# Two graph layers over 16 batches: the list path of the kernel issued in text order

## The chip, the core and the metric

The kernel runs as one program on one core of a Trainium2 chip. The metric is the device time of one execution in microseconds (us). The engines are called by the names of the profile: PE (matmuls; PEld is its weight load), DVE (the vector engine), ACT (the scalar engine), POOL (GpSimd, which here only issues indirect DMAs: gathers and scatters of rows by a list of row numbers) and SP (which issues the plain DMAs).

## The reference

There are B = 16 batches of N = 1024 nodes with C = 64 channels, and a weighted adjacency of 1024 x 1024 for each batch, with self-loops; its expected degree falls with the node's number. Both layers begin with a layer norm and a relu, and add their result to x. Layer 0 is a mean over neighbours weighted by the adjacency. Layer 1 removes some neighbours of nodes with more than ten (each k-th one, in both directions), takes for each node and channel the weighted 0.25, 0.5 and 0.75 quantiles over the neighbours that are left, adds the node's own value, and applies a perceptron of 64, 128 and 64 channels.

```python
h = relu(layernorm(x))
x = x + matmul(adj / clip(sum(adj, 2), 1), h)          # layer 0
h = relu(layernorm(x))                                  # layer 1
adj_d = dilate(adj)            # nodes with over 10 neighbours lose each skip-th
sv = sort(where(adj_d > 0, h of neighbours, big))       # per node and channel
agg = 0.25 * q(0.25) + 0.5 * q(0.5) + 0.25 * q(0.75)    # interpolated quantiles
x = x + (relu((h + agg) @ W1 + b1) @ W2 + b2) * mask
```

## The kernel before, in words

**Layer 0 (a batch at a time).** `front` (L303) norms x, and for each of eight blocks of 128 rows loads the block of the adjacency (L329, 512 KB, tile `at`), takes its signs on ACT (L331), turns them on DVE into numbered marks (L332, L333) and finds the eight largest of each of four segments with MAX8 (L336): these are the neighbour lists, in `rec`. PE transposes the block (L341), ACT copies it out of PSUM (L342). `product` (L356) multiplies half a batch by h (16 matmuls, L358), ACT copies the result (L363) and PE turns it back; it runs inside block 4 and at the start of `back`. `back` (L382) writes the new h to the table `tab` and to `own` in DRAM, sorts the nodes by degree (L408 to L433) and permutes the lists by matmuls with one-hot tiles (L438, L444) into `rec_g`.

**Lists of a group.** A group is four batches. `group` (L652) lays the permuted lists on 128 partitions (nodes of like degree together, 31 columns), makes the neighbour indices, and writes for the largest nodes what was dropped (scatters at L757). It then makes ten jobs, one for each list length from 15 down to 1 (L768). `long_lists` (L777) does the same for the four classes of longest lists (88, 31, 24 and 20 neighbours), over all batches, after a gather of whole adjacency rows (`lat`).

**A job** has T columns of nodes with n = length + 1 places each. `fetch` (L611) issues T x n gathers on POOL (L481): the node's own row into `S`, and each neighbour's row into the tile `places` (`lplaces` for the long lists). `sort` runs `aggregate` (L486) on DVE: it marks what was removed (`rem`, `gone`, `ok`, L491 to L502), makes the quantile weights (`wu` on DVE, two ACT instructions L472 and L473, then `w` on DVE, L476), sorts by a network of minimum and maximum operations (L531) and multiplies by the weights (L544, tile `prod`). `layers` is the perceptron: PE (L572), ACT (L577), PE (L579), ACT (L581), PE (L585, L588), ACT into `y` (L590). `add` (L629) adds x on DVE, `store` (L593) scatters T rows of the output from POOL (L595). `pipeline` (L634) runs step s: fetch of job s + 2, stores of job s - 2, layers of job s - 1, sort of job s, add of job s - 1. A job's tile `places` has three buffers.

**Order.** The program is written as Python generators that yield an estimated cost; `weave` (L850) takes its next piece from the stream that has used the smallest share of its weight. But this text order is only a priority: the framework's scheduler then reorders each engine's instructions by its own model, and each engine runs its queue in that order. A sort is cut into pieces of about 8 us by estimate (L520). Groups 0 and 1 are woven with layer 0; when layer 0 is over, groups 2 and 3 are woven with the long lists (L901 to L907).

Of the kernel before, what the change touches and what calls it, by code (L numbers as in the profile page):

```python
# [1 line left out]

# [5 lines left out]
F32 = mybir.dt.float32  # L8
# [17 lines left out]
GB = 4  # L26
# [11 lines left out]
WAIT = "wait"  # L38
AHEAD = 2
# [77 lines left out]
def kernel(  # L117
# [26 lines left out]
    list_path(tc, x, adj, nodemask, w1, b1, w2, b2, out, go)  # L144
# [7 lines left out]
def list_path(ctx, tc, x, adj, nodemask, w1, b1, w2, b2, out, go):  # L152
# [27 lines left out]
    diff = consts.tile([P, P], I32, name="diff")  # L180
# [23 lines left out]
    place1 = consts.tile([P, P], F32, name="place1")  # L204
    nc.vector.tensor_scalar(place1, col[:, :P], 1.0, None, op0=OP.add)
    cls_i = consts.tile([P, CLS, NT], I32, name="cls_i")
# [46 lines left out]

    first = keep.tile([REC, len(LONG), B, LSUB], HF, name="first")
# [40 lines left out]

    def load(pool, b):
# [6 lines left out]
    def front(pool, st, following):  # L303
# [17 lines left out]
        st["att"] = []  # L321
        for t in range(NT):
# [5 lines left out]
            at = pool.tile([P, N], F32, name="at", bufs=3)  # L328
            nc.sync.dma_start(at, adj[b, blk, :])  # L329
# [5 lines left out]
            for s in range(NSEG):  # L335
                nc.vector.max(out=rec[:, t, 8 * s:8 * s + 8], in_=segs[:, s, :])  # L336
            for h2 in range(2):
# [7 lines left out]
                )  # L345
            if t == BPH:
                product(pool, st, 0)
# [4 lines left out]
            yield 2.6  # L352
# [29 lines left out]
    def back(pool, st, rec_g):  # L382
# [5 lines left out]
        for _ in range(3):  # L388
            yield 0.0
# [45 lines left out]
        for hf in range(2):  # L435
            perm = pool.tile([P, NT, HALF], HF, name="perm", bufs=1)
            for t in range(NT):
# [3 lines left out]
                )  # L441
            pr = ps_m.tile([P, HALF], F32, name="pm")
# [14 lines left out]
            yield 2.9  # L457
# [28 lines left out]
    def aggregate(pool, n, T, A, S, keys, node):  # L486
# [32 lines left out]
        for op, ai, aj, dist, run in ops:  # L519
            if cost > 8.0:  # L520
                yield cost
                cost = 0.0
# [8 lines left out]
            nc.vector.tensor_tensor(dst, a, c, op)  # L531

# [6 lines left out]
        for copy in range(2):  # L539
            for run in runs_of([k for k in range(count) if at[k] == copy]):  # L540
# [6 lines left out]
                )  # L547
        yield cost + 0.4 + count * T * C * 1.05e-3
# [13 lines left out]
    def perceptron(terms, mask, T):  # L562

        R = terms[0][0].shape[1]
        y = mlp.tile([P, T, CO], F32, name="y", bufs=2)
# [27 lines left out]
    def store(y, T, idx):  # L593
        for t in range(T):
            ins = nc.gpsimd.indirect_dma_start(  # L595
                out=out_rows, out_offset=bass.IndirectOffsetOnAxis(ap=idx[:, t:t + 1], axis=0),
                in_=y[:, t, :], in_offset=None,
            )

            for other in scatters:  # L600
                tc.declare_no_dep(ins.ins, other, reason="rows of their own")
            scatters.append(ins.ins)

    class Job:


        def __init__(self, pool, n, T, keys, idx, node, mask, nodes_i, table, mine, name="places",
                     bufs=3):
            self.__dict__.update(locals())

        def fetch(self):  # L611
# [19 lines left out]
        def store(self):  # L631
            store(self.y, self.T, self.nodes_i)
# [566 lines left out]
```

## Time and profile before

| | us |
|---|---|
| median of 8 runs | 2077.95 |
| lowest and highest run | 2057.58 and 2094.01 |
| the profiled execution | 2065.86 |
| its span, first to last instruction | 2064.1 |
| DVE busy in the span | 1289.8 (62%), 4747 instructions |
| POOL busy | 1120.2 (54%), 940 instructions |
| PE busy, PEld | 868.7 (42%), 523.0 (25%) |
| ACT busy | 436.3 (21%) |

Busy is time in which the engine ran an instruction of the program; instructions of DVE overlap by some 70 ns, and what is counted is the union. POOL leaves 0.30 us between two DMA instructions that wait for nothing, so its busy share understates how full its queue is. In the lines, L481 is the line of the helper that issues every gather; `places<-tab,idx` are the gathers of group jobs (496), `lplaces<-tab,lidx` those of the long lists (163), `S<-own,nodes_i` the nodes' own rows (124 and 4), `out_dram<-y,nodes_i` the stores (124 and 4). "Remote" in a wait means that no instruction or DMA in the profile was seen to end it.

### The profile page before, as it was taken

What the parts mean: (1) busy time and instruction counts of PE and PEld (TensorE: products, weight loads), DVE (VectorE), ACT (ScalarE), POOL (GpSimd) and SP (SyncE); (2) the same over time, 40 slices, a digit from 0 to 9 for tenths busy, and PEclk for the clock granted to TensorE, in tenths of its full rate; (3) what the DMA queues carried; (4) which work ended last, traced back from release to release, by engine and by line L of the source; (5) the groups of instructions that cost most, each with busy time, mean ns of one, the idle gap of its engine ahead of it and who ended that gap; (6) DMA issues with size and microseconds to landing.
All of it is one profiled execution on the core that took longest, in us unless ns stands there. A gap on an engine that the chain in (4) does not pass through costs nothing.

```text
span 2064.1 us, 15523 instructions
## 1 busy us (share of the span) xinstructions
PE 868.7 (42%) x3724; PEld 523.0 (25%) x3724; DVE 1289.8 (62%) x4747; ACT 436.3 (21%) x1010; POOL 1120.2 (54%) x940
## 2 busy tenths in 40 slices
PE   6886256457773754479300010001225215121165
PEld 3443123233541422245100000001113104121044
DVE  9998588537777785677694111179656475555172
ACT  6663134123443432233100000000001100000011
POOL 0002637653327444742327777664888888378753
PEclk9997578567886876778555555555556556555566
DMA  6554244142344432331111111100111101000100
GB/s 198 157 154 116 59 113 124 37 117 66 89 113 103 118 96 64 103 86 24 35 45 25 27 27 27 25 15 9 25 21 22 22 11 23 13 20 15 32 17 14
DMA packets 116516, 124.32 MB, mean 60 GB/s; under 512 B 84242, under 2 KB 84370, under 8 KB 116418
## 3 DMA queue, kind: packets, MB, share of 16 engines
q1 hardware_dynamic: 85730, 84.15, 14.8%
q0 software_dynamic: 30688, 39.11, 9.1%
q8 instruction: 31, 0.51, 0.1%
q14 instruction: 67, 0.55, 0.1%
HBM read 106.27 MB, written 16.92 MB: 60 GB/s over the span
## 4 chain that ended last, share of the span: by engine, by line
POOL 25%; DVE 21%; PE 21%; issue 16%; another core or an unknown queue 8%; DMA 4%; ACT 3%; POOLq 0%; SPq 0%; DVEq 0%; ACTq 0%
POOL places L481 14%; PE pm L358 8%; POOL lplaces L481 7%; DVE other L531 4%; PE pm L444 4%; PE pt L341 4%; PE pt L572 2%; DVE places L531 2%; DVE rec L336 2%; POOL out_dram L595 2%; POOL S L481 2%; DVE lplaces L531 1%; DMA at<-in_adj_dram 1%; DMA places<-tab,idx 1%
## 5 line engine op out<-in xcount | busy, mean ns | idle before, releaser
L481 POOL DMA_INDIRECT places<-tab,idx x496 | 663.9, 1339 | 387.0 <-DVE prod L544 177.7
L572 PE MATMUL pt<-ident,prod 128*128 128x128 f32 (+1 forms) x736 | 160.0, 373 | 660.0 <-DVE prod L544 329.3
L572 PEld LDWEIGHTS pt<-ident,prod 128*128 128x128 f32 (+1 forms) x736 | 128.0, 254 | 702.7 <-issue 241.2
L358 PE MATMUL pm<-att,h 128*65 128x512 f32 x512 | 242.8, 621 | 3.3 <-issue 1.8
L595 POOL DMA_INDIRECT out_dram<-y,nodes_i x124 | 128.8, 1039 | 150.5 <-issue 53.3
L341 PE MATMUL pt<-ident,at 128*128 128x128 f32 x1024 | 164.8, 307 | 70.7 <-ACT att L342 27.4
L336 DVE MAX8 rec<-sg 128x8 f16<-128x256 f16 x512 | 188.7, 413 | 2.8 <-DVE base L430 1.1
L481 POOL DMA_INDIRECT lplaces<-tab,lidx x163 | 155.3, 953 | 49.7 <-issue 49.4
L481 POOL DMA_INDIRECT S<-own,nodes_i x124 | 145.0, 1169 | 60.3 <-issue 31.9
L331 ACT ACTIVATE sg<-at 128x1024 f16<-128x1024 f32 x128 | 135.8, 1061 | 154.8 <-DVE rec L336 112.3
L341 PEld LDWEIGHTS pt<-ident,at 128*128 128x128 f32 x1024 | 132.3, 158 | 112.0 <-issue 59.4
L342 ACT COPY att<-pt 128x512 f32<-128x512 f32 x256 | 141.0, 588 | 78.1 <-PE pt L341 36.2
L444 PE MATMUL pm<-perm,rec 128*34 128x512 f16 x256 | 98.1, 498 | 86.4 <-DVE perm L438 55.4
L531 DVE TENSOR_TENSOR places<-other 128x128 f32<-128x128 f32 (+6 forms) x264 | 86.6, 350 | 58.5 <-remote 54.1
L531 DVE TENSOR_TENSOR other<-places 128x128 f32<-128x128 f32 (+6 forms) x276 | 93.0, 350 | 35.5 <-remote 26.8
L590 ACT ACTIVATE y<-ps_small,recs 128x64 f32<-128x64 f32 x124 | 30.8, 313 | 372.5 <-DMA out_dram<-y,nodes_i 259.8
L579 PE MATMUL pm<-ot,w_sb 128*128 128x128 f32 (+3 forms) x112 | 51.5, 558 | 134.0 <-ACT ot L577 71.4
L358 PEld LDWEIGHTS pm<-att,h 128*65 128x65 f32 x512 | 69.8, 144 | 140.4 <-issue 133.5
L476 DVE TENSOR_TENSOR w<-wu 128x16 f32<-128x16 f32 (+12 forms) x44 | 7.7, 176 | 152.9 <-ACT wu L473 95.8
L481 POOL DMA_INDIRECT gat_rows<-in_adj_dram,nodes_i x4 | 4.0, 1012 | 178.3 <-DVE over L686 173.4
L629 DVE TENSOR_TENSOR y<-y,S 128x64 f32<-128x64 f32 (+4 forms) x44 | 15.1, 344 | 134.9 <-DMA out_dram<-y,nodes_i 69.8
L333 DVE TENSOR_TENSOR sg<-sg,rev 128x1024 f16<-128x1024 f16 x128 | 87.1, 683 | 12.0 <-issue 7.5
(194 smaller groups left out, 1687.6 us busy)
## 6 DMA issues: line engine op xcount, KB each, us to landing
at<-in_adj_dram SPq DMA_DIRECT2D x128, 512.0 KB
places<-tab,idx POOLq DMA_INDIRECT x496
tab<-h SPq DMA_DIRECT2D x16, 264.0 KB
xt<-in_x_dram SPq DMA_DIRECT2D x16, 256.0 KB
own<-x SPq DMA_DIRECT2D x16, 256.0 KB
own<-h SPq DMA_DIRECT2D x16, 256.0 KB
lplaces<-tab,lidx POOLq DMA_INDIRECT x163
S<-own,nodes_i POOLq DMA_INDIRECT x124
```

Source lines behind the costliest of these rows:

```text
L331: nc.scalar.activation(sg, at, AF.Sign, accum_out=total[:, t:t + 1])
L333: nc.vector.tensor_tensor(sg, sg, rev, OP.mult)
L336: nc.vector.max(out=rec[:, t, 8 * s:8 * s + 8], in_=segs[:, s, :])
L341: nc.tensor.transpose(pt[:, q * P:(q + 1) * P], at[:, c0:c0 + P], ident)
L342: nc.scalar.copy(att[:, h2 * BPH:(h2 + 1) * BPH, k * P:(k + 1) * P], pt.rearrange("p (q i) -> p q i", i=P),)
L358: nc.tensor.matmul(po[:C + 1, :], st["h0"][:, q, :], st["att"][hf][:, q, :], start=(q == 0), stop=(q == NT - 1),)
L444: nc.tensor.matmul(pr[:REC, :], rec[:, t, :], perm[:, t, :], start=(t == 0), stop=(t == NT - 1))
L481: nc.gpsimd.indirect_dma_start(out=dst, out_offset=None, in_=src, in_offset=bass.IndirectOffsetOnAxis(ap=idx, axis=0),)
L531: nc.vector.tensor_tensor(dst, a, c, op)
L572: nc.tensor.matmul(pt[:term.shape[1], i * P:(i + 1) * P], term, ident, start=(k == 0), stop=(k == len(terms[t]) - 1),)
L579: nc.tensor.matmul(ph[:, :M], w1_sb[:R, :], ot[:R, :M], start=True, stop=True)
L595: ins = nc.gpsimd.indirect_dma_start(out=out_rows, out_offset=bass.IndirectOffsetOnAxis(ap=idx[:, t:t + 1], axis=0), in_=y[:, t, :], in_of ...
```

## The change

The scheduler's reordering is switched off for the list path (`manual_schedule`): every engine issues its instructions in the order of the program's text. That order is written anew:

- Layer 0 yields after each MAX8; rows of the adjacency are loaded two blocks ahead, at the end of a block. `front` and `back` of neighbouring batches run by weights 24 and 14 instead of in turn.
- A sort yields after about 0.9 us of operations by estimate (`PIECE`) instead of 8. After each 0.8 us of sorting operations (`BREATH`) DVE gets a memset of one element per partition (`breathe`).
- The ten jobs of a group go into one queue for all groups, in an order that pairs long lists with short ones. One `pipeline` runs all 40. The cost of a piece of a sort is now counted in POOL's time: 1.27 us for each gather or store of the step, shared out over the sort's pieces.
- In a step the stores are dealt among the fetches (`transfers`), a store first; after a store with no fetches left POOL gets a small memset.
- The lists of a group have weight 0, which puts them before everything else as soon as four more batches are done. While layer 0 runs, the jobs of all groups that have lists are dealt against it at 730 to 480. When it is over come the lists of group 3, all four long lists, and then the long jobs against the rest of the group jobs at 440 to 300. The long jobs fetch two ahead.
- Some setup tiles share space, and `y` has three buffers instead of two.

```diff
+BREATH = 0.8
+PIECE = 0.9
...
-    list_path(tc, x, adj, nodemask, w1, b1, w2, b2, out, go)
+    with tc.manual_schedule():
+        list_path(tc, x, adj, nodemask, w1, b1, w2, b2, out, go)
...
+        def __call__(self, cost):
+            self.since += cost
+            if self.since > BREATH:
+                nc.vector.memset(idle, 0.0)
+                self.since = 0.0
...
                 nc.vector.max(out=rec[:, t, 8 * s:8 * s + 8], in_=segs[:, s, :])
+                if s < NSEG - 1:
+                    yield 0.9 if s == 0 else 0.42
...
+            if t + 2 < NT:
+                rows.append(load_rows(pool, b, t + 2))
+            elif following is not None:
+                following["rows"].append(load_rows(pool, following["b"], t + 2 - NT))
...
-            yield 2.6
+            yield 0.42
...
         product(pool, st, 1)
-        for _ in range(3):
-            yield 0.0
+        yield 4.0
...
+                if t % 2:
+                    yield 0.7
...
-            if cost > 8.0:
+            if cost > PIECE:
                 yield cost
                 cost = 0.0
...
             nc.vector.tensor_tensor(dst, a, c, op)
+            breathe(0.07 + len(run) * T * C * 1.05e-3)
...
-        y = mlp.tile([P, T, CO], F32, name="y", bufs=2)
+        y = mlp.tile([P, T, CO], F32, name="y", bufs=3)
...
+            self.cost = 2.5 + (2 * n * T * C * 1.05e-3) + sum(
+                0.15 + len(run) * T * C * 1.05e-3 for *_, run in network(n)[0]
+            )
...
+    def transfers(fetch, store):
+
+        fetch = list(fetch.fetches()) if fetch is not None else []
+        store = list(store.stores()) if store is not None else []
+        while fetch or store:
+            if store:
+                store.pop(0)()
+                if not fetch:
+                    nc.gpsimd.memset(turn, 0.0)
+            for _ in range(-(-len(fetch) // (len(store) + 1))):
+                fetch.pop(0)()
+
+    def pipeline(jobs, total, ahead, by_pool=True):
+
+
+        for s in range(-ahead, total + 2):
+            fetch = store = None
+            if s + ahead < total:
+                while len(jobs) <= s + ahead:
+                    yield WAIT
+                fetch = jobs[s + ahead]
+            if 0 <= s - 2:
+                store = jobs[s - 2]
+            time = 1.27 * ((fetch.n * fetch.T if fetch else 0) + (store.T if store else 0))
+            transfers(fetch, store)
+            if 1 <= s <= total:
                 jobs[s - 1].layers()
-            if s < J:
-                yield from jobs[s].sort()
-            if 1 <= s <= J:
+            if 0 <= s < total:
+                for cost in jobs[s].sort():
+                    yield time * cost / jobs[s].cost if by_pool else cost
+            else:
+                yield time if by_pool else 0.1
+            if 1 <= s <= total:
                 jobs[s - 1].add()
-            yield 0.2
+            if by_pool:
+                progress["sorted"] = max(s + 1, 0)
...
-        for ts in classes:
+
+        half = len(classes) // 2
+        mixed = [ts for pair in zip(classes[:half], classes[:half - 1:-1]) for ts in pair]
+        for ts in mixed + classes[half:len(classes) - half]:
...
-            yield from alternate(front(pool, st, following), ending)
+            yield from streams((front(pool, st, following), 24.0), (ending, 14.0))
...
+            while progress["batches"] < (g + 1) * GB or progress["sorted"] < (g - 1) * per_group:
                 yield WAIT
             yield from group(g, records[g])
-            yield from pipeline(todo[g], AHEAD)
+            progress["groups"] = g + 1
...
+        yield from long_lists(pool, 0)
+        while progress["groups"] < NG:
+            yield WAIT
+        for l in range(1, len(LONG)):
             yield from long_lists(pool, l)
...
-        weave((lay0, 480.0), (groups(records, (0, 1)), 270.0))
+        layer0 = batches(pool, records)
+        emit(layer0, lambda: progress["batches"] == GB)
+        emit(
+            streams((lists, 0.0), (layer0, 480.0), (jobs, 730.0)),
+            lambda: progress["batches"] == B,
+        )
     with tc.tile_pool(name="long", bufs=1) as pool:
-        def rest():
-            yield from group(2, records[2])
-            yield from group(3, records[3])
-            progress["dropped"] = True
-            yield from pipeline(todo[2] + todo[3], AHEAD)
-        weave((longs(pool), 440.0), (rest(), 270.0))
+        emit(streams(
+            (lists, 0.0), (longs(pool), 0.0),
+            (pipeline(long_jobs, len(LONG), 2, by_pool=False), 440.0), (jobs, 300.0),
+        ))
```

## The prediction

> **What bounds the kernel now.** I read first the table of busy times by stage: layer 0 of the first five batches, the rest of layer 0 with groups 0 and 1, and all that follows; then one stretch of the last.
>
> ```profile
> core 0: us, PE busy (x) PEld busy (x) DVE busy (x) ACT busy (x) POOL busy (x), PEclk, DMA share, GB/s
> 0.00:170.00 170.00, 138.54 (x612) 70.64 (x612) 156.92 (x565) 101.93 (x199) 1.91 (x9) 0.94 0.60 167
> 170.00:990.00 820.00, 498.25 (x2074) 273.75 (x2072) 573.58 (x2108) 270.18 (x602) 396.84 (x371) 0.75 0.34 87
> 990.00:2064.00 1074.00, 231.90 (x1042) 178.56 (x1041) 559.28 (x2075) 64.15 (x209) 721.43 (x561) 0.54 0.11 23
> 1140.00:1300.00 160.00, 11.89 (x36) 8.63 (x36) 23.00 (x113) 2.56 (x10) 121.30 (x128) 0.50 0.14 27
> ```
>
> No engine is full after 170 us. DVE is idle 246 us of the second stage (820 - 574) and 515 us of the third (1074 - 559). From 1140 to 1300 POOL gathers 128 rows of long lists in a train and DVE works 23 us of 160. The third stage, with half the group jobs and all the long lists, has the most to give.
>
> The timeline of POOL (start, duration) shows what sorting does to gathers, that of DVE what a train of gathers does to sorting:
>
> ```profile
> 1644.48 11.14 POOL L481 DMA_INDIRECT places<-tab,idx  x1 [0.30 <-DMA places<-tab,idx]
> 1655.92 13.70 POOL L481 DMA_INDIRECT places<-tab,idx  x1 [0.30 <-issue]
> 1669.93 7.39 POOL L481 DMA_INDIRECT places<-tab,idx  x1 [0.30 <-issue]
> ```
>
> ```profile
> 1148.73 0.29 DVE L531 TENSOR_TENSOR places<-other 128x128 f32<-128x128 f32 x1 [6.12 <-remote]
> 1150.13 0.29 DVE L531 TENSOR_TENSOR places<-other 128x128 f32<-128x128 f32 x1 [1.11 <-remote]
> ...
> 1154.33 0.15 DVE L281 TENSOR_SCALAR half<-half 128x1 int32<-128x1 int32 x1 [3.58 <-remote]
> 1155.73 0.16 DVE L284 TENSOR_TENSOR far<-far,lrec 128x1 f32<-128x1 f32 x1 [1.25 <-DVE half L281]
> ```
>
> An undisturbed gather takes 0.94 us and 0.30 to the next. These three lie under unbroken rows of two-input operations. In the second view DVE waits for its own earlier result (those waits are for its own semaphore), and gets it 1.4, 2.8 or 4.2 us late while gathers follow each other. The two engines shut each other out, and whoever is unbroken wins.
>
> Last the list of waits (total us, times, longest):
>
> ```profile
> ACT y L590 <- DMA out_dram<-y,nodes_i: 259.8, 12, 75.6
> ...
> DVE w L476 <- ACT wu L473: 95.8, 17, 21.7
> ...
> DVE y L629 <- DMA out_dram<-y,nodes_i: 69.8, 2, 51.3
> ...
> DVE w L476 <- ACT wu L472: 52.5, 4, 18.3
> ```
>
> Stores stand in POOL's queue behind fetches of later jobs, so `y` comes free late (first and third line); and DVE waits for the quantile weights behind whatever ACT has in front of them: with 4.6 from other causes 152.9 us over 44 jobs, 3.5 each.
>
> **The change, part by part.**
>
> *Work that stays, and what is added.* POOL keeps 923 gathers and stores and 8 scatters: 931 x 1.25 = 1164 us of queue if nothing shuts it out. DVE keeps 1290. Following the sorting networks through the rule of `breathe`, a group's jobs get 74 memsets and the long jobs 280: 576 in all. A memset of one element takes 0.059 us in the setup (L223): 34 us. POOL's memsets after last stores are a few tenths each: nothing.
>
> *The breath.* In the second stage, where MAX8 and other one-input work lies between the sorts, 248 `places` gathers took 263.2 us (1.06 each); from 1450 to 1900 us 141 took 265.6 (1.88). So an operation with one input lets gathers in, and a memset has none. I count gathers at 1.25 us again in the last stage. That matters only where POOL is last.
>
> The Trainium skill (SBUF — State Buffer, Who interferes with whom) has it that a DVE operation with two SBUF inputs holds only the pair's read side and, by inference, leaves descriptor writing alone. Then breaths would be 34 us for nothing. The 13.70 us gather speaks against it. The same section lets one-input operations outside the two-port modes pass GpSimd, as the 1.06 does.
>
> *First stage.* Five fronts and four backs, as before: DVE 157 us. In text order ACT's copy of `product` (L363) stands before the signs of the next block; PE needs 16 x 0.43 = 6.9 us for it, during which DVE has some 3 us of its own. I charge 4 us a batch: 170 + 20 = 190.
>
> *Second stage.* Layer 0 has 467 units of estimated cost left (11 fronts of 21.5, 12 backs of 19.2), so at 480 to 730 the jobs get 710 units of POOL's estimate, of 4 x 186 x 1.27 = 945: three quarters, and with fetches two steps ahead 28 jobs of 40 are sorted, eight more than now, and group 2's lists are made. By successive starts in the trace the 40 group sorts hold DVE 375 us (9.4 each), a group's lists 14, the long lists 67, the long sorts 264. So DVE has 574 + 8 x 9.4 + 14 + 207 breaths x 0.059 = 675 us; POOL 557 x 1.25 = 696. Neither covers the other, so what DVE waits for counts in full:
> - `w`. `layers` of the job before now always stands in ACT's queue before `wu`, and nothing of DVE between. For T = 4 that chain took in the trace 1482.2 (first PE) to 1492.9, then 0.9 for `y` and 0.6 for `wu`: 12 us; about 104 for the ten jobs of a group, 10.4 each. Layer-0 pieces that fall between the last product and the next step cover some 2, and ACT runs ahead of DVE. Between 3.5 (the row of waits) and 10.4 I take 4.5, nearer the row that was measured: 28 x 4.5 = 126.
> - Other layer-0 waits, 117 us now (sg, ln_v, base, perm, rec): finer pieces put other work between producer and consumer, text order takes away the freedom to pass: 60 (0 to 120).
> - Its own results and landings, 46 and 25 now: 40.
> Together 675 + 226 = 901, ending at 1091.
>
> *Third stage.* Group 3's lists and four long lists come first, 81 us of DVE. The gather of `lat` has one buffer, so the fourth goes out when DVE begins the third list, about 68 us in; behind it stand the 89 fetches of the first long job, 89 x 1.25 = 111: landed at 182. The first piece of that sort follows at once in DVE's text, so DVE idles some 85 us there. What is left on DVE then: 559 - 14 - 75 + 369 breaths x 0.059 - 81 = 411. POOL has 267 x 1.25 = 334 us meanwhile, hidden. Waits for `w`: 12 x 4.5 + 4 x 4 = 70. The stores that held `y` (70 on DVE) now go out two steps later at the head of a step: 0. The end, from the last product through perceptron, add, store and the final flag, is 15 us as now. Together 182 + 411 + 70 + 15 = 678.
>
> Sum: 190 + 901 + 678 = 1769 us of span, 1771 for the execution (2065.86 - 2064.1 lies around it). The profiled execution is 0.6% under the median; on the median's scale 1781. I say 1775.
>
> **The rivals.**
> 1. *Both engines stay full* (17%). If finer pieces hide the waits on ACT, the second stage is POOL's 696 or DVE's 675 plus little, 715, the first 175, the third 182 + 411 + 15 = 608: about 1500. For it: in the first stage DVE is already busy 157 of 170 us. Against it: nothing stands between `wu` and `w` in the text.
> 2. *The full chain is waited for* (15%): 10.4 us for 40 jobs instead of 4.5 adds 236: 2010. For it: single waits reach 21.7 us.
> 3. *The breath gives the port away, and DVE pays* (12%). Each breath lets a gather in; the two-input operation behind it then waits out that gather (0.94 us), as the DVE view shows. If three of four breaths cost that, 576 x 0.75 x 0.94 = 406: about 2180, slower. It decides from (2066 - 1771) / 576 = 0.51 us a breath. Against it: in the second stage gathers and sorts already lie together, and waits on "remote" by sorting operations are under 20 us.
> 4. *The breath does nothing* (5%): the excess over 0.94 (228 us, summed over 159 gathers over 1.1 us in the trace) comes back where 334 us of POOL lie under 411 of DVE: 334 + 228 - 411 = 150 more, 1920.
>
> **How the numbers follow.** The forecast has 51%; its own range is 1640 to 1920: both ends of the other waits (-60, +60), `w` at 3.5 or 7 (-44, +110). About 1% is what a measurement of this kernel can tell from no change. Faster by over 1%: forecast, rivals 1 and 4, and most of rival 2: 0.83. Within 1%: 0.04, where rivals 2 and 3 come out near 2066. Slower: most of rival 3 and the end of 2, 0.13. The range leaves out the far half of rival 1 and rival 3: 1540 to 2030.
>
> **What would show it.** Right: at 990 us more than 20 group sorts done; no gather above 3 us in the last stage; no wait of `y` on `out_dram` of any size; waits of `w` on ACT near 196 us; one idle stretch of 85 us on DVE before the first long sort. Wrong: DVE busy over 85% after 190 us (rival 1); `w` waits above 350 us (rival 2); waits on "remote", or of a sorting operation for another, that begin right behind a memset and sum to over 250 us (rival 3); gathers over 5 us under sorts with breaths between (rival 4).

## The result, and the profile after

The changed kernel is slower: 2578.02 us (median of 10 runs, 2562.61 to 2608.02) against 2078.83 us for the kernel before, measured beside it. The ratio is 1.243, with a 95% interval of 1.2387 to 1.2472. The prediction was 1775 us, between 1540 and 2030: the sign was wrong. Ratios, here and below, compare only executions in the faster of the two states that a kernel is met in, while each time is the median of all its runs, so the two need not divide exactly. The profiled execution has a span of 2552.9 us.

First the page's busy times and, of its 40 slices, those of DVE:

```profile
PE 1016.1 (40%) x3724; PEld 626.1 (25%) x3724; DVE 1410.1 (55%) x5316; ACT 432.6 (17%) x1009; POOL 940.9 (37%) x955
...
DVE  6666754545645537357245454676065477853164
```

POOL's busy time fell, as the change was meant to make it (1120.2 us before, 940.9 now). DVE's busy time rose by 120 us, of which the memsets are 33.6, and its idle time rose from 774 to 1143 us. In the kernel before DVE was busy 157 of the first 170 us; now none of the slices of layer 0, the first 26, reaches eight tenths.

PE changed too, which the prediction did not reckon with: the same 3724 matmuls were busy 868.7 us before and 1016.1 now. The clock granted to PE fell from 0.658 to 0.621 of full speed on average, and a transpose of the adjacency (L341, now L368) took 374 ns instead of 307. So every chain that leads through PE got longer. Whether the slower clock comes from the gaps in PE's work, and how much of the loss it carries, was not tested.

The stages end where the lists of the first group and of the last one are begun. This view gives span, then the busy time of each engine, the clock granted to PE and the traffic for each stretch; the third stretch is the lists of the last group and of the long nodes, with the first long fetch:

```profile
core 0: us, PE busy (x) PEld busy (x) DVE busy (x) ACT busy (x) POOL busy (x), PEclk, DMA share, GB/s
0.00:270.00 270.00, 163.08 (x617) 84.42 (x618) 180.69 (x568) 96.22 (x195) 1.97 (x9) 0.81 0.36 102
270.00:1657.00 1387.00, 679.62 (x2404) 407.05 (x2402) 737.47 (x2690) 296.64 (x686) 550.27 (x557) 0.64 0.23 58
1657.00:1873.00 216.00, 9.67 (x27) 6.22 (x26) 95.11 (x229) 2.73 (x8) 93.73 (x98) 0.50 0.11 26
1873.00:2553.00 680.00, 163.76 (x678) 128.40 (x678) 396.82 (x1832) 37.04 (x120) 294.92 (x292) 0.55 0.08 16
```

The first stage took 270 us (forecast 190), the second 1387 (901), the third 896 (678). The first is the cleanest witness: it has no gathers and no sorts in it, only layer 0 in text order, and it already took 80 us more than forecast. In the second stage neither DVE (737 of 1387) nor POOL (550) is anywhere near full.

Next the waits of DVE (waiting instruction, what ended the wait, total us, times, longest), whole span:

```profile
DVE w L508 <- ACT wu L505: 369.1, 29, 45.5
DVE sg L357 <- ACT sg L356: 237.0, 50, 18.1
DVE rem L523 <- DMA lplaces<-tab,lidx: 93.7, 1, 93.7
DVE w L508 <- ACT y L624: 70.6, 5, 37.2
DVE sg L357 <- issue: 63.4, 12, 20.9
DVE w L508 <- ACT wu L504: 31.9, 4, 16.1
DVE other L563 <- issue: 28.2, 16, 5.1
DVE w L508 <- issue: 26.3, 6, 5.3
```

All of `w` comes to 498.0 us (152.9 before, 196 forecast), all of `sg` to 300.5. Before, the sign had cost DVE little more than this:

```profile
DVE sg L332 <- ACT sg L331: 21.6, 5, 17.9
```

The one wait of 93.7 us is the landing of the first long fetch, which the prediction had at 85.

How one such wait is made up, the longest, is seen in three timelines (start, duration, engine, line, idle time before). DVE's, where it stops for 45 us with a whole sort queued behind:

```profile
739.00 0.20 DVE L500 TENSOR_TENSOR wu<-col_f,q 128x39 f32<-128x39 f32 x1
784.68 0.17 DVE L508 TENSOR_TENSOR w<-wu 128x13 f32<-128x13 f32 x1 [45.48 <-ACT wu L505]
```

And ACT's for the same time:

```profile
732.02 0.41 ACT L588 COPY prod<-S 128x256 f32<-128x256 f32 x1
774.71 0.58 ACT L611 COPY ot<-pt 128x512 f32<-128x512 f32 x1 [42.28 <-remote]
777.46 0.69 ACT L615 ACTIVATE hid<-pm,b_sb 128x512 f32<-128x512 f32 x1 [2.17 <-PE pm L613]
783.24 0.93 ACT L624 ACTIVATE y<-ps_small,recs 128x64 f32<-128x64 f32 x4 [5.09 <-PE ps_small L622]
784.04 0.25 ACT L504 ACTIVATE wu<-wu 128x39 f32<-128x39 f32 x1
784.32 0.33 ACT L505 ACTIVATE wu<-wu,wt 128x39 f32<-128x39 f32 x1
```

And PE's, the transposes that the first of these copies waits for:

```profile
733.81 4.57 PE L606 MATMUL pt<-ident,prod 128*128 128x128 f32 x24 [1.18 <-issue]
```

DVE's `wu` was ready for ACT at 739.20, and the two ACT steps on it take 0.6 us. But in ACT's text three steps of the perceptron of the job before stand ahead of them, and the first waits for PE. DVE can take nothing else either, since its own text has `w` next. The queues alone do not make this wait so long, though: PE's last transpose of that job ended at 738.4 in the trace, and ACT went on at 774.7, 36.3 us later. Such late signals are taken up at the end.

The waits of `w` are not all of one kind. Seven of over 30 us make 269 of the 498 us, and the other 37 jobs wait 6.2 us on average. Of the seven, the two longest (45.5 and 41.3 us) hold signals of PE that came 36.3 and 31.4 us late, and two in the last stage (37.7 and 39.4 us) stand behind an ACT step into `y`, which itself waits for a store to free a buffer:

```profile
ACT y L624 <- DMA out_dram<-y,nodes_i: 40.1, 1, 40.1
```

For the other of these two the profile records no end of the wait of `y` (36.1 us), but `y` began 2.3 us after a store was issued on a semaphore that it waits for.

### The profile page after: what moved, and what is told of

It is laid out like the page before. It is cut to its first block, busy times and chain, and to the rows that moved or that the text cites. A ratio compares the mean times of both kernels' runs of the same rounds, so it can differ in the third digit from the quotient of the medians.

```text
span 2552.9 us, 15931 instructions
## 1 busy us (share of the span) xinstructions
PE 1016.1 (40%) x3724; PEld 626.1 (25%) x3724; DVE 1410.1 (55%) x5316; ACT 432.6 (17%) x1009; POOL 940.9 (37%) x955
## 4 chain that ended last, share of the span: by engine, by line
DVE 33%; PE 23%; issue 18%; POOL 10%; another core or an unknown queue 8%; ACT 7%; DMA 1%; DVEq 0%; ACTq 0%; SPq 0%; POOLq 0%
PE pm L389 6%; DVE other L563 6%; POOL lplaces L513 6%; PE pt L606 6%; DVE rec L361 3%; DVE places L563 3%; POOL places L513 3%; DVE lplaces L563 3%; ACT sg L356 2%; PE pm L476 2%; DVE sg L358 2%; PE ps_small L619 2%; PE pt L368 2%; PE ps_small L622 2%
## 5 line engine op out<-in xcount | busy, mean ns | idle before, releaser
L513 POOL DMA_INDIRECT places<-tab,idx x496 | 501.8, 1012 | 169.9 <-issue 142.9
L606 PE MATMUL pt<-ident,prod 128*128 128x128 f32 (+1 forms) x736 | 184.8, 420 | 760.8 <-DVE prod L577 524.2
L606 PEld LDWEIGHTS pt<-ident,prod 128*128 128x128 f32 (+1 forms) x736 | 147.0, 291 | 794.5 <-DVE prod L577 316.0
L508 DVE TENSOR_TENSOR w<-wu 128x16 f32<-128x16 f32 (+12 forms) x44 | 7.9, 179 | 498.0 <-ACT wu L505 369.1
L368 PE MATMUL pt<-ident,at 128*128 128x128 f32 x1024 | 206.3, 374 | 167.0 <-ACT att L369 81.6
L368 PEld LDWEIGHTS pt<-ident,at 128*128 128x128 f32 x1024 | 173.2, 196 | 189.2 <-ACT att L369 94.5
L361 DVE MAX8 rec<-sg 128x8 f16<-128x256 f16 x512 | 191.6, 417 | 6.9 <-issue 2.6
L357 DVE TENSOR_TENSOR sg<-sg,off_diag 128x128 f16<-128x128 f16 x128 | 28.1, 219 | 300.5 <-ACT sg L356 237.0
L611 ACT COPY ot<-pt 128x128 f32<-128x128 f32 (+3 forms) x56 | 22.5, 402 | 742.6 <-PE pt L606 587.9
L513 POOL DMA_INDIRECT S<-own,nodes_i x124 | 123.5, 996 | 37.8 <-issue 37.5
L613 PE MATMUL pm<-ot,w_sb 128*128 128x128 f32 (+3 forms) x112 | 63.1, 659 | 137.3 <-ACT ot L611 96.3
L563 DVE TENSOR_TENSOR other<-places 128x128 f32<-128x128 f32 (+6 forms) x276 | 93.7, 351 | 17.3 <-issue 12.9
L468 DVE TENSOR_SCALAR perm<-col_h,pos 128x512 f16<-128x512 f16 x256 | 73.1, 353 | 44.1 <-remote 24.7
L563 DVE TENSOR_TENSOR places<-other 128x128 f32<-128x128 f32 (+6 forms) x264 | 86.5, 351 | 13.9 <-remote 9.3
```

What stands on the lines that cost most here:

```text
L368: nc.tensor.transpose(pt[:, q * P:(q + 1) * P], at[:, c0:c0 + P], ident)
L468: nc.vector.tensor_scalar(perm[:, t, :], col_h[:, hf * HALF:(hf + 1) * HALF], pos[:, t:t + 1], None, op0=OP.is_equal,)
L513: nc.gpsimd.indirect_dma_start(out=dst, out_offset=None, in_=src, in_offset=bass.IndirectOffsetOnAxis(ap=idx, axis=0),)
L606: nc.tensor.matmul(pt[:term.shape[1], i * P:(i + 1) * P], term, ident, start=(k == 0), stop=(k == len(terms[t]) - 1),)
L613: nc.tensor.matmul(ph[:, :M], w1_sb[:R, :], ot[:R, :M], start=True, stop=True)
```

## The experiments

Each kernel was timed beside the kernel before on the same chip; the ratio is to that. The chips differ: the kernel before took 2075 us beside the new text under the scheduler, the two single hoists and the POOL memset; 2048 beside both hoists, ACT alone, DVE alone and all but ACT; 2044 beside ACT with DVE, the changed kernel without memsets and the old one with them; 2058 beside PE alone, POOL alone, the three engines and the new text under the scheduler without memsets; and 1911 beside the three kernels of experiment 5.

**1. Is it the text order at all?** The new text, with the scheduler's reordering left on:

```diff
-    with tc.manual_schedule():
-        list_path(tc, x, adj, nodemask, w1, b1, w2, b2, out, go)
+    list_path(tc, x, adj, nodemask, w1, b1, w2, b2, out, go)
```

> The new text with the scheduler's reordering left on. Queue theory: the scheduler moves the weights and the signs forward as it did before, waits of w under 200 us and of the signs under 60, time 1800-2100. Late signals: they depend on how POOL's gathers follow each other, which the new text sets; over 200 us of late waits stay and the time is over 2300. Dearer VectorE (breaths, small pieces): busy stays near 1400 us and the time is 100 us over the kernel before, about 2180.

Measured 2081.32 us, ratio 0.994 (0.986 to 1.003): no difference from the kernel before. So the whole price belongs to the text order, and the rest of the change (the new mixture, small pieces, memsets, stores among fetches, a third buffer for `y`) is worth nothing net when the scheduler places it. Its waits of `w` come to 95.2 us in all and those of the sign to 81.4, above the 60 expected. Its page has the busy times, and the longest of the waits that had carried the loss:

```profile
PE 896.1 (43%) x3724; PEld 551.9 (27%) x3724; DVE 1298.6 (62%) x5316; ACT 433.9 (21%) x1010; POOL 970.3 (47%) x955
```

```profile
DVE w L507 <- ACT wu L504: 76.1, 12, 37.8
DVE sg L356 <- ACT sg L355: 76.0, 11, 18.9
```

The same 5316 DVE instructions are busy 1298.6 us here and 1410.1 us in text order. The sums of their durations differ by only 22 us (1681 and 1703); the other 90 us are overlap. 5016 of them begin before the one ahead has ended in the scheduled kernel, 3807 in text order. Of the 1509 that do not in text order, 1313 wait for DVE's own semaphore, that is for an earlier result of DVE. They are not the sorting networks: of 1906 operations of L563 only 118 begin late (78 in the scheduled kernel). They are short chains in which each step needs the one ahead, such as the sign's product and the first MAX8 of each block (L358 and L361, 258 together) and the small steps of the marks and weights of a job (L495 to L534); the scheduler puts something independent between.

**2. Is it one badly placed step?** Two hoists in the text, singly and together. The perceptron of the last job behind the first piece of the next sort:

```diff
+            pieces = jobs[s].sort() if 0 <= s < total else None
+            first_cost = next(pieces) if pieces and by_pool else None
             if 1 <= s <= total:
                 jobs[s - 1].layers()
```

> The perceptron of the job before is issued behind the first piece of the next sort (for the group jobs; the long jobs stay as they are), so the two ACT steps that make the weights stand ahead of it. Queue theory (DVE's small steps wait because ACT's queue has work in front that waits for PE): waits of w fall from 498 us to under 180 (what is left is that of the four long jobs and the bare latency), time 2578 to 2190-2330. Rival, late signals (PE's and DVE's semaphores arrive late while POOL runs a train of gathers, 306 us of waits that end over 1 us after the work was done): the late PE signals only hit another step, time over 2450. Rival, dearer VectorE (busy 1410 instead of 1290 us): no change beyond 2%.

Measured 2517.88 us, 1.220 (1.198 to 1.242; two runs). And the sign of a block issued on ACT before the transposes and copies of the block ahead of it:

```diff
+        ahead = sign(0)
         for t in range(NT):
...
-            nc.scalar.activation(sg, at, AF.Sign, accum_out=total[:, t:t + 1])
+            sg = ahead
...
+            if t + 1 < NT:
+                ahead = sign(t + 1)
             for h2 in range(2):
```

> The sign of a block of the adjacency is issued on ACT ahead of the copies of the block before, instead of behind them. Queue theory: waits of DVE for the signs fall from 300 us to under 80, time 2578 to 2300-2400. Late signals: the copies still come late, the waits move on to the residual and to the product, time over 2500. Dearer VectorE: no change.

Measured 2498.11 us, 1.210 (1.193 to 1.227; two runs). Neither time is the one that the theory of the queues had named; the first lies in the range of its rival, late signals. The waits of DVE in the first of the two,

```profile
DVE sg L357 <- ACT sg L356: 374.5, 55, 26.0
DVE sg L357 <- issue: 96.8, 12, 15.6
...
DVE w L508 <- ACT wu L505: 82.9, 36, 35.5
DVE w L508 <- issue: 80.7, 4, 78.4
```

and in the second (its lines lie 6 to 8 further down):

```profile
DVE w L516 <- ACT wu L513: 359.3, 27, 45.5
DVE sg L363 <- ACT sg L351: 107.9, 25, 18.0
...
DVE w L516 <- ACT y L632: 82.7, 4, 47.9
DVE w L516 <- issue: 69.4, 7, 39.4
DVE sg L363 <- issue: 58.0, 8, 19.0
```

The wait that was hoisted shrinks, by 318 us for `w` and 135 for `sg`, and the other grows, `sg` by 171 and `w` by 42: the gain is 60 and 80 us. Together:

> Both hoists together: the layers of the last group job behind the first piece of the next sort, and each block's sign ahead of the transposes and copies of the block before. If the price of the text order is a few badly placed steps (w and sg, 498 + 300 us of DVE's waits in the changed kernel), both go and the time is 2578 less some 550 us, about 2030. If the steps only take turns at being last in ACT's line, the gains do not even add: one alone gave 60 us and the other 80, so 2430 to 2500, and the trace shows a third DVE wait (the copies behind the sorting permutation, x1's product, or the sign still) grow by 100 us or more. Simple addition of the two gains is 2438.

Measured 2405.8 us, 1.175 (1.166 to 1.183). The gains add (1.243 less 0.023 and 0.033 would be 1.187), so the hoists do not merely undo one another. But the gain is 0.068 of 2079, some 140 us, of the 798 that `w` and `sg` had cost by their rows. `w` fell by 321 us, to 177, while DVE's idle time fell by 163, from 1143 to 980: about half was handed on. The sign is still the longest wait, at 335 us in all.

**3. Whose order?** The order can be fixed engine by engine, with an otherwise identical text; one line of the kernel differs, as for ACT:

```diff
-    with tc.manual_schedule():
+    with tc.manual_schedule(engines={mybir.EngineType.Activation}):
```

> The changed kernel with the text order kept on ACT alone; all others are the scheduler's. Theory A (ACT's line alone is enough): 2400 to 2600, with DVE's waits for w at 300 us or more. Theory B (DVE's order) and theory C (PE's order): 2080 to 2200. In between, 2200 to 2400: ACT's line costs by itself, but the fixed order of DVE or PE adds to it.

> The changed kernel with the text order kept on DVE alone; PE, ACT, POOL and SP are the scheduler's. Theory A (ACT's line): near the scheduled version, 2080 to 2200. Theory B (DVE's fixed order): near the changed kernel, 2480 to 2600. In between, 2250 to 2450, would mean that the price needs two engines whose orders are both fixed.

> The changed kernel with the text order kept on PE, DVE, POOL and SP, and ACT alone left to the scheduler. Nothing else differs, so it tells whose order costs. Theory A (ACT's line is the coupler: what DVE needs from ACT stands behind ACT steps that wait for PE): most of the 497 us between the changed kernel under the scheduler (2081) and in text order (2578) comes back, 2080 to 2250. Theory B (DVE's own fixed order costs, since it can take no other work while one result is late): 2480 to 2580, with DVE's waits for w and sg little changed. Theory C (PE's fixed order holds the chain up whatever ACT does): also 2450 to 2580, but with ACT waiting for PE in the chain of waits.

> The changed kernel with the text order kept on ACT and DVE together; PE, POOL and SP are the scheduler's. The single orders cost 5.3% (ACT) and 8.1% (DVE) of the old kernel, all five together 24%. Theory D (each of the two lines alone finds other work while the other waits; fixed together they wait for one another): 1.20 to 1.25. If the two prices only add: 1.13 to 1.15, and the rest, some 10%, is PE's, POOL's and SP's order. If PE's order is the third that is needed: 1.14 to 1.19.

> The changed kernel with the text order kept on ACT, DVE and PE; POOL and SP are the scheduler's. ACT and DVE fixed gave 1.177, all five 1.243. If PE's line is the third that counts (a transpose or a perceptron step behind products of other work): 1.22 to 1.25, and POOL and SP cost nothing. If the rest is POOL's order (a late scatter ahead of fetches) or SP's: 1.165 to 1.195.

> The changed kernel with the text order kept on PE alone. With the others free: 0.99 to 1.02 if PE's line costs only together with ACT's; 1.03 to 1.08 if PE's fixed order costs by itself as ACT's (1.053) and DVE's (1.081) do.

| in text order | us | ratio | interval |
|---|---|---|---|
| none | 2081.3 | 0.994 | 0.986 to 1.003 |
| PE | 2072.0 | 1.010 | 1.006 to 1.014 |
| ACT | 2152.0 | 1.053 | 1.044 to 1.062 |
| DVE | 2218.5 | 1.081 | 1.073 to 1.090 |
| ACT, DVE | 2403.3 | 1.177 | 1.170 to 1.184 |
| ACT, DVE, PE | 2493.6 | 1.214 | 1.207 to 1.220 |
| PE, DVE, POOL, SP | 2287.4 | 1.111 | 1.100 to 1.123 |
| all five | 2578.0 | 1.243 | 1.239 to 1.247 |

No one queue is the cause. ACT's line, which I held for the coupler, costs 5.3% alone and 13.2 points on top of the other four; the expectation that it alone would reach 2400 fell, and leaving ACT alone to the scheduler brought 2287, less back than the 2080 to 2250 of that theory. DVE's costs 8.1% (2218 us, between the ranges of its cases), ACT's and DVE's together 17.7%, more than their sum of 13.4. PE's line costs 1.0% alone and 3.7 points on top of those two, so it costs mainly together with them. The other 2.9 points are POOL's and SP's.

DVE's part can be read from the page of the kernel with DVE alone in text order. The 112 us of busy time are all there, while its idle time is 807 us against 780 in the kernel with no order fixed, so they are over half of its price.

```profile
PE 925.9 (42%) x3724; PEld 575.8 (26%) x3724; DVE 1410.8 (64%) x5316; ACT 439.8 (20%) x1010; POOL 958.4 (43%) x955
```

With all but ACT in text order, the longest wait of `w` is a third of what it was, and that of the sign about half (in all 162 and 142 us):

```profile
DVE w L508 <- ACT wu L505: 115.8, 32, 22.9
DVE sg L357 <- ACT sg L356: 111.6, 18, 19.0
```

POOL alone was run as well:

> The changed kernel with the text order kept on POOL alone, the scheduler on the others: stores dealt among the fetches as written. If POOL's written order is worth anything by itself: 0.96 to 0.985. If it is as good or bad as the scheduler's: 0.985 to 1.005. If a store that waits for its `y` holds up the fetches behind it: 1.01 to 1.05.

Measured 2183.97 us, 1.062 (1.057 to 1.066). It looks like the third case expected, if larger, but the trace offers another reason. With DVE left to the scheduler, a run of the one-element memsets was taken out of the sorts and put into DVE's queue in a row, about 160 of them from 1414 to 1636 us, just where POOL gathers the first long lists:

```profile
1421.10 0.06 DVE L269 MEMSET idle<- 128x1 f32 x1 [1.34 <-DVE idle L269]
1422.50 0.06 DVE L269 MEMSET idle<- 128x1 f32 x1 [1.34 <-DVE idle L269]
```

They all write one tile, so each waits for the one ahead, and most get that signal 1.34 us late while the gathers go on. In this kernel the memsets have 222 us of idle time before them, in the one with no order fixed 18, in text order 1.2. How much of the loss they make was not tested, so this run does not price POOL's order; that stays open.

**4. The memsets and the gathers.** Without memsets in the changed kernel (`BREATH` set beyond reach):

> The changed kernel in text order without the 570 one-element DVE memsets. POOL is not what bounds it (941 us of 2553), so slower gathers should cost little: the gathers' mean goes back from 1.01 to 1.3 us or more and POOL's busy time from 941 to 1150 or more, while the time stays within 2540 to 2640. If the memsets' 34 us lie on DVE's path and nothing else changes, 2545; if the late landings of the first long fetch show (it has nothing beside it, 110 us for 88 gathers), some 40 us more than now, 2620.

Measured 2577.1 us where the kernel before took 2044, 1.260 (1.252 to 1.268): with them it is 1.243, so in text order they gain about 1.4%. The two ratios are from two chips. The gathers of `places` took 1119 ns on average without them, 1012 with, and single ones show why (POOL's timeline of the kernel without memsets):

```profile
2135.59 26.81 POOL L513 DMA_INDIRECT S<-own,nodes_i  x1 [0.30 <-issue]
```

From 2136 to 2163 us DVE was busy 26.90 us of 27, with two-input operations alone, and this gather ended only 0.8 us after the first gap in the row of over 25 ns, one of 104 ns at 2161.6. 15 gathers of that kernel took over 3 us, two of the changed one, the longest 6.39. The memsets do what they are for; what it is worth is another matter. In the old text, under the scheduler:

> The old kernel, old text, the scheduler's order, with only the one-element memsets put into the sorting. In it POOL is busy 584 us of the 789 between the first and the last gather of the long lists, at 1339 ns a gather. If the slow gathers bound that stage, they come down to about 1010 ns, POOL's busy time falls from 1120 to some 950 us, and the time falls by 60 to 140 us, 1940 to 2020. If DVE or the chain of a job bounds it, the gathers are faster, and the time stays within 2050 to 2115 (up to 34 us dearer for the memsets). If the scheduler moves the memsets out of their places, the gathers stay at 1.2 us or more and the time at 2060 to 2115.

Measured 2096.41 us, 1.023 (1.017 to 1.029): slower, if by little. The gathers fell from 1339 to 1085 ns, and POOL's busy time in the stretch of the long lists from 584 to 469 us, while that stretch shrank only from 789 to 765 us: POOL was not what bounded it. In the new text under the scheduler, without memsets:

> The changed text under the scheduler without the one-element memsets: a candidate to beat both kernels. In the old text the memsets cost 2.3% though the gathers got shorter, so without them the new text (0.994 with them) should give 0.965 to 0.985. If in the new text POOL's gathers are nearer to the path, the memsets earned what they cost, and it gives 0.99 to 1.02.

Measured 2053.57 us, 0.996 (0.991 to 1.000), against 0.994 with them: no difference. And a second small memset, on POOL between gathers, to see whether its unbroken trains delay the other engines' signals:

```diff
                 fetch.pop(0)()
+                nc.gpsimd.memset(turn, 0.0)
```

> A memset of one element on POOL after every gather of a step, so that gathers do not follow each other directly. Queue theory: POOL is not on the path, time within 2% of 2578. Late signals: the waits that end over 1 us after the work was done fall from 306 us to under 100, time 2250-2450.

Measured 2583.2 us, 1.251 (1.229 to 1.274): nothing gained.

**5. Is the wait for the weights itself on the path?** Instead of moving it, these kernels make it impossible. The two ACT steps on `wu` are done by DVE:

```diff
-        nc.scalar.activation(u, u, AF.Abs)
-        nc.scalar.activation(u, u, AF.Relu, bias=wt0, scale=-QUANTILES[0][1])
+        nc.vector.scalar_tensor_tensor(u, u, -1.0, u, op0=OP.mult, op1=OP.max)
+        nc.vector.tensor_scalar(u, u, 1.0, -QUANTILES[0][1], op0=OP.min, op1=OP.mult)
...
-        nc.vector.tensor_tensor(w, u[:, 0, :, :], u[:, 1, :, :], OP.add)
+        nc.vector.scalar_tensor_tensor(
+            w, u[:, 0, :, :], 4 * QUANTILES[0][1], u[:, 1, :, :], op0=OP.add, op1=OP.add
+        )
```

In the changed kernel:

> The changed kernel in text order, with the two ACT steps of the weights (44 x 238 and 333 ns) done on DVE instead, two more instructions of about 0.21 us each per job, 18 us in all. DVE then asks ACT for no weights at all, so the 498 us of waits at w can't exist. If they were a price of their own: 2578 - 498 + 18, a ratio of 1.00 to 1.03. If ACT's line is merely waited for at the next place (the sign, y, the copies behind the permutation), as when the layers were moved behind the first piece: 1.17 to 1.22. Half way, 1.09 to 1.14, is what leaving ACT to the scheduler gave (1.111).

Measured 2085.22 us where the kernel before took 1911.04, ratio 1.092 (1.088 to 1.095), the half-way case. Its stages and its longest waits:

```profile
0.00:269.00 269.00, 161.08 (x618) 83.44 (x619) 181.02 (x570) 96.30 (x195) 2.39 (x10) 0.81 0.36 102
269.00:1357.00 1088.00, 655.55 (x2398) 395.67 (x2396) 749.31 (x2743) 281.00 (x630) 558.81 (x556) 0.68 0.29 74
1357.00:2087.00 730.00, 171.46 (x710) 134.50 (x710) 496.20 (x2093) 31.73 (x96) 396.11 (x390) 0.54 0.11 23
```

```profile
DVE sg L357 <- ACT sg L356: 293.8, 53, 23.3
DVE rem L525 <- DMA lplaces<-tab,lidx: 93.8, 1, 93.8
DVE y L669 <- ACT y L626: 58.3, 3, 38.7
```

The first stage, which has no weights in it, is as long as in the changed kernel (269 and 270 us), and the second and third are 299 and 166 us shorter. The waits of `sg` did not grow (293.8 us, 300.5 in all before). That speaks for the wait for the weights as a price of its own, at least in part on the path: hoisting the perceptron had left the demand on ACT in place, and this removes it. The size can't be read exactly, because this chip is the one on which the kernel before takes 1911 us, and the changed kernel as it is was not run there. If the chip gave it what it gave the kernel before, 168 us of the 465 would be the chip's, and some 300 the edit's (an estimate). This chip's traces also show none of the late signals of the last section. If all of the changed kernel's 310 us or so of them had been on the path, some 155 would be left for the edit (an estimate too).

The same edit in the old kernel and in the new text under the scheduler without memsets:

> The old kernel and the scheduler's order, with the weights' two ACT steps on DVE: a candidate to beat both. In the old profile DVE waits 153 us at w and would pay 18 us. If these waits are on the path: 0.93 to 0.96. If the time goes to the next wait of the same job (the landing of the gathers, y): 0.98 to 1.01.

> The changed text under the scheduler without memsets (0.996), with the weights' two ACT steps on DVE. If the waits at w are on the path there as well: 0.94 to 0.97. If not: 0.98 to 1.01.

The old kernel: 1921.91 us, 1.007 (1.005 to 1.010); there the 153 us of waits went into others, above all `y` (304 us on ACT's `y`, 65 in the profile before, which is from another chip). The new text: 1808.75 us, 0.947 (0.944 to 0.949). This is faster than both kernels. It has the new text, the scheduler's order and the weights on DVE, and no memsets. Beside it on the same chip, the kernel in text order with the same weights (and with memsets) takes 2085 us, 15% more, 276 us. So text order costs that much even where DVE never waits for the weights and no signal is over 1 us late; the sign alone is waited for 293.8 us there, and 5.1 us under the scheduler. The edit alone gives nothing in the old text on the same chip; the new text alone gave 0.996, but on another chip, so how its 5.3% divides between edit, text and chip stays open. What DVE waits for most now is POOL, whose gathers are slow again (1290 ns, 1012 in the changed kernel):

```profile
DVE rem L524 <- DMA places<-tab,idx: 310.1, 22, 50.5
```

The old text in text order wasn't tried: by its text, its fetches and stores could wait for one another in a queue that nobody reorders.

## Why the prediction was wrong

The forecast span was 1769 us, the measured one is 2553, 784 more. Of these 86 are DVE busy (1324 forecast, 1410), and 698 are DVE idle (445 forecast, 1143): `w` 302, the sign and the permutation 265 (80 forecast with the first stage's 20, 300.5 + 44.1 measured), the landing of the long fetch 9, and many small waits 122.

- **The step that failed first is the size of `w`.** The prediction saw that the perceptron's steps now always stand ahead of `wu`, and counted the chain at 10.4 us. Then it took 4.5 us, "nearer the row that was measured", 3.5 us a job. That row was measured under a scheduler which had already put other work into the gap. In text order it measured 498 / 44 = 11.3 us a job. That is not simply the chain: 37 jobs wait 6.2 us on average, and seven long waits, among them those behind late signals and behind `y`'s waits for a store, make the rest. The stores that hold `y` were another term of the sum, put at 0, and in the last stage they stood behind two waits of `w`, 77 us together.
- **The second is "other layer-0 waits", 60 us.** The prediction said in one breath that text order takes away the freedom to pass and that finer pieces put work between, and let the two cancel. The sign was put down at 4 us a batch in the first stage and at nothing of its own later. The first stage alone took 80 us more than forecast; it has 66.6 us of waits at `sg` and 24 us more of DVE's busy time. The hoists bear out the reason: an ACT step that DVE asks for stands behind steps that wait for PE, and when one is moved forward, the waits for the other grow.
- **"DVE keeps 1290" was wrong** by 86 us after the memsets are counted. It took instructions to cost what they cost in the old order. Their busy time depends on what stands ahead of them: against the scheduled kernel 90 us of overlap are lost where dependent ones follow one another, and the instructions are 22 us longer in sum.
- **Right as mechanism and size:** the gathers came back near their pitch (1012 ns of work and 0.30 us between, 1.31 us a gather for 1.25), though two in the last stage took over 3 us; 570 memsets of 59 ns, 33.6 us, for 576 and 34; 27 of the jobs' `y` adds stand before the last group's lists, 28 forecast; the idle stretch before the first long sort 93.7 us for 85; waits of DVE's `y` on a store are gone (69.8 us before), though ACT's side kept the two of 40.1 and 36.1 us in the last stage.
- **The range.** The prediction's own range, 1640 to 1920, does not follow from its parts: 1775 less 60 and 44 is 1671, and with 60 and 110 more it is 1945. That changes nothing here.
- **The rivals.** Both engines full did not happen. Rival 3, in which each breath costs DVE a gather, is refuted in text order: the instructions right behind the 570 memsets wait 36.8 us in all, 20 of them for ACT's sign, where this rival had 406. (The 1.34 us where memsets follow one another, in experiment 3, are late signals, and not this.) Rival 4 is refuted by the gathers' mean; and the inference of the Trainium skill that spoke for it (SBUF — State Buffer, Who interferes with whom: operations with two SBUF inputs leave descriptor writing alone) has the 26.81 us gather against it, as it had the 13.70 us one; whether it is the writing of descriptors that waits, or the reading of the row numbers, which lie in a tile, no run here separates. Rival 2 came nearest on `w`, and its sign showed (498 us, for over 350), but it charged `w` alone and came to 2010. With the sign's 265 and DVE's 86 beside it, it would have ended at 2361 and on the right side.
- The time saved on POOL was real, 180 us of its busy time, and bought nothing. POOL was at 54% before; experiment 1 shows that, placed by the scheduler, what the new text gains and what it costs come to nothing.

## What to carry over

A wait read from a scheduled trace is what the scheduler could not hide, not what the step costs: when the order is fixed by hand, price each wait by its full chain, and every engine that a chain passes through gets such a price. Fixing several in-order queues at once can cost more than the sum: here ACT and DVE cost 5.3% and 8.1% alone and 17.7% together. If a wait can't be passed any more, take the demand away (do the small step on the engine that needs it) rather than move the producer up, which here moved about half of the wait to the next step that the same queue owes.

## What the runs showed of the hardware

While POOL issues gathers one behind the other, other engines' semaphores are seen late in most of these traces. I took each wait of over 1.5 us on PE, ACT or DVE and compared the increment that ended it with the end of the last instruction ahead of it that makes such an increment. In the changed kernel some 40 waits were for an increment over 1 us late, about 310 us in all, mostly PE's, up to 36.3 us (the one at 774.7 above). In that one POOL issued gathers and stores without a break until 768.7, and ACT went on 6.0 us after the last of them. In the kernel before there are some 90, about 370 us, many of them DVE's own result in steps of 1.4 us; in the new text under the scheduler some 100, about 600 us. Ends of matmuls are modelled and some of their records can be missing, so a single one may have another cause. The scheduled kernel has the most of them and is no slower than before, and in the first stage of the changed kernel, which already lost time, there are none, so they do not explain the loss as a whole. They may still cost more where no queue can pass them by: ACT idled 142.5 us at `ot` before four of them in the changed kernel, and 81 of these lie behind the end of PE's work. A POOL memset between gathers left them (some 40 waits, about 320 us).

In the three traces from the chip on which the kernel before takes 1911 us there is not one such wait. These three also hold a record of every increment (of DVE's in the text-order one 3085, for 3083 instructions that make one), while in the changed kernel's trace about one in eight is missing from the first gather on (2596 records for 2979), and it is much the same in the other traces. So late signals and missing records go together here. Whether one causes the other, whether that is why this chip is some 7% faster with the same kernel, and what the text order would cost on it without the edit, wasn't measured.
